# Recorded set-up, source exponentials spread by broadcast transfers, node tiles by halves and re-weighted stream keys, in a scheduled graph-attention kernel

## Chip, cores, metric

One core of one Trainium2 chip. The metric is device time of one launch in microseconds (us), the median of several runs; less is better. "Period" below is the time between the same point of two following batches in a trace (the first transpose of the last layer's attention input; batches 1 to 15).

## The reference

Sixteen independent batches of 1024 nodes with 256 channels and one adjacency matrix shared by all. Three graph-attention (GAT) layers (4, 1 and 1 heads), then 8-head attention with a feed-forward part, each on a normalised input with a residual.

```python
def gat(h, adj, W, a, alpha):                 # one head
    q = h @ W
    e = (q @ a_src)[:, None] + (q @ a_dst)[None, :]
    e = where(e >= 0, e, alpha * e)           # leaky
    return elu(softmax(where(adj > 0, e, -inf)) @ q)

for l in range(3):                            # H = 4, 1, 1
    x = x + gat_l(relu(layernorm(x)), adj)
x = x + block(relu(layernorm(x)))             # 8-head masked attention, norm, two products, norm
```

The kernel writes exp(leaky(s + d)) as a product of exponentials, so that one VectorE instruction makes a tile of weights: max(row, column) times mask. `row` holds the source exponentials of 512 nodes, the same in all 128 partitions. How `row` gets there is what the change is about.

## The kernel before

All work is recorded first, item by item, with an engine, a booked duration and the buffers read and written. A list scheduler then plays the program in its own clock, decides the order on every engine, and emits one in-order program per engine. All DMA transfers are issued by one queue (SyncE), in that order.

```python
PASS = {"pe": 0.22, "act": 0.18, "dve": 0.15, "pool": 0.13, "dma": 2.0}   # booked hand-over

def add(self, engine, us, emit, w=(), r=(), modes=("full", "full")):
    x = Work(engine, us, frozen(emit), self.base + self.pos / self.per, modes)   # key
    if engine == "pe":
        self.pos += us
    ...
def choose(e):             # lowest key among what is ready at free[e]; an item that opens
    ...                    # a ring buffer counts as ready only when a buffer is free
free[e] = at + us          # the engine's clock moves by the booked time alone
```

The rows, by four transposes on TensorE and a copy on ScalarE, for each of 12 rows of a batch:

```python
def spread(hf, h):
    g, row = r_bank.new(), r_row.new()
    pe(0.109 * TH, lambda: transposes(
            lambda k: g.t[:, k * P : (k + 1) * P],
            lambda k: e3[:, hf * TH + k, H + h : H + h + 1].to_broadcast([P, P]), TH), ...)
    act(act_us(HALF), lambda: nc.scalar.copy(row.t, g.t), [row], [g])
    return row
...
for h in range(0, H, 2):                       # layer 0: pairs of heads
    row = [spread(hf, h + u) for u in range(2)]   # the ring of rows has two buffers
```

In the same stretch of a batch the queries and keys of the attention are split into a high and a low part and stacked by small transfers, 128 of 64 KB per batch:

```python
act(act_us(HALF), lambda: nc.scalar.copy(hi.t.bitcast(F32R), sc.t), [hi], [sc])
dve(tt_us(HALF), lambda: nc.vector.tensor_sub(lo.t, sc.t, hi.t), [lo], [sc, hi])
for a in range(4):
    part = ((hi, hi, lo, lo), (hi, lo, hi, lo))[keys][a]
    for r in range(HG):
        dma(0.4, lambda: nc.sync.dma_start(              # <- booked at 0.4 us
                stack.t[a * D3 : (a + 1) * D3, r, at : at + HALF],
                part.t[r * D3 : (r + 1) * D3, :]), ...)
```

Streams set the order of preference: an item's key is its batch's number plus the TensorE time booked so far in its stream, divided by the stream's constant (`GATS, ATTENTION, FEED, AHEAD = 148.0, 110.0, 300.0, 1.0`), and the lowest key is preferred. The set-up (weights, mask) is emitted ahead of the schedule. (Cuts are marked by "..."; comments behind # are mine.)

## Time and profile before

| | before |
|---|---|
| time, median of 3 | 4728.55 us (4726.73 to 4729.57) |
| TensorE busy | 4574.2 of 4728.9 us |
| period of a batch | 286.7 us |
| start of the first attention weights | 63.1 us |

The prediction shows the lines that carry the bound. A line of this view has: line of the kernel, engine, operation, output<-inputs, shapes, count | busy us, mean ns | idle time of that engine just before them and what ended it.

```profile
L606 DVE SCALAR_TENSOR_TENSOR pt<-row,e,mask 128x512 f32<-128x512 f32 x1536 | 1071.5, 746 | 70.9 <-ACT e L540 41.7 <-ACT row L598 20.0 <-PE bank L712 5.9
...
L1024 PE MATMUL sc<-qs,ks 128*128 128x512 f32 x2048 | 822.7, 474 | 52.6 <-ACT pa L1037 20.1 <-DMA qs<-lo 16.8 <-issue 10.3
...
L702 PE MATMUL bank<-pt,qb 128*64 128x512 f32 x2048 | 529.3, 616 | 10.4 <-DVE pt L606 10.3
```

L1024 is the attention score. L606 makes the weight tiles: VectorE idled 71 us ahead of them, 20 of that for rows.

### The profile page before, as it was taken

The numbers are of one execution on the slowest core, as the hardware profiler recorded it, in microseconds if no ns is written. First come the engines' busy times: TensorE is split into PE (matmuls) and PEld (weight loads), VectorE is DVE, ScalarE is ACT, GpSimd is POOL, SyncE is SP. The second block draws the span as 40 slices with busy tenths as digits, with TensorE's granted clock in tenths as the row PEclk, the third lists the DMA queues.
The fourth block names the chain that finished last, engine by engine and source line by source line (L and its number), as shares of the span: only waits on it lengthen the run. The fifth ranks groups of instructions, "written<-read, shape, count | busy, mean of one in ns | idle before, by whom it ended". The sixth has DMA issues, their size and how long they took to land.

```text
span 4728.9 us, 67592 instructions
## 1 busy us (share of the span) xinstructions
PE 4574.2 (97%) x24898; PEld 2458.2 (52%) x24898; DVE 3400.3 (72%) x6403; ACT 2441.3 (52%) x5065; POOL 288.5 (6%) x455
## 2 busy tenths in 40 slices
PE   6899999999999999999999999999999999999997
PEld 2646456364554646546364563645546465463643
DVE  6476776867677776776777768676777767768756
ACT  2445546454554645546455464545546455464554
POOL 0000001000000000001000000000000000000000
PEclk9999999999999999999999999999999999999998
DMA  2011211102121121211212111021211212101121
GB/s 79 18 49 31 67 37 45 46 23 68 36 61 30 36 57 33 71 32 33 55 32 67 37 46 45 23 68 36 63 29 35 59 32 72 33 26 50 32 70 41
DMA packets 151234, 213.02 MB, mean 45 GB/s; under 512 B 37232, under 2 KB 71536, under 8 KB 150896
## 3 DMA queue, kind: packets, MB, share of 16 engines
q1 hardware_dynamic: 150896, 208.62, 16.2%
q8 instruction: 199, 3.26, 0.3%
q14 instruction: 139, 1.14, 0.1%
HBM read 40.70 MB, written 33.55 MB: 16 GB/s over the span
## 4 chain that ended last, share of the span: by engine, by line
PE 84%; DVE 5%; DMA 4%; SPq 4%; ACT 2%; issue 1%; POOL 0%; DVEq 0%; ACTq 0%
PE bank L632 19%; PE bank L936 19%; PE sc L1024 12%; PE bank L702 9%; PE bank L529 6%; PE bank L480 6%; PE bank L712 5%; SPq L871 3%; PE sc L850 3%; PE bank L1107 3%; DMA out_dram<-xr 2%; DVE pt L606 1%; DVE stf L423 1%; PE sc L480 1%; ACT pa L1037 1%
## 5 line engine op out<-in xcount | busy, mean ns | idle before, releaser
L1037 ACT ACTIVATE pa<-sc 128x512 f32<-128x512 f32 x2048 | 1120.4, 604 | 1018.7 <-PE sc L1024 864.4
L1045 DVE TENSOR_TENSOR pa<-pa,mask 128x1024 f32<-128x1024 f32 x1024 | 1233.4, 1221 | 446.2 <-ACT pa L1037 441.6
L606 DVE SCALAR_TENSOR_TENSOR pt<-row,e,mask 128x512 f32<-128x512 f32 x1536 | 1071.5, 746 | 70.9 <-ACT e L540 41.7
L632 PE MATMUL bank<-qb,pt 128*128 128x257 f32 x4096 | 967.2, 384 | 5.8 <-DVE pt L606 2.7
L632 PEld LDWEIGHTS bank<-qb,pt 128*128 128x128 f32 x4096 | 767.7, 190 | 234.1 <-issue 116.7
L1024 PE MATMUL sc<-qs,ks 128*128 128x512 f32 x2048 | 822.7, 474 | 52.6 <-ACT pa L1037 20.1
L1024 PEld LDWEIGHTS sc<-qs,ks 128*128 128x128 f32 x2048 | 364.3, 188 | 470.4 <-issue 165.1
L936 PE MATMUL bank<-pa,va 128*32 128x512 f32 x4096 | 546.4, 605 | 0.0
L702 PE MATMUL bank<-pt,qb 128*64 128x512 f32 x2048 | 529.3, 616 | 10.4 <-DVE pt L606 10.3
L936 PE MATMUL bank<-pa,ones 128*32 128x512 f32 x4096 | 534.1, 592 | 0.0
L529 PE MATMUL bank<-w_aug,hT 128*128 128x259 f32 (+1 forms) x1536 | 382.4, 392 | 3.7 <-ACT qb L547 2.3
L529 PEld LDWEIGHTS bank<-w_aug,hT 128*128 128x128 f32 x1536 | 284.4, 191 | 119.0 <-issue 43.5
L432 POOL TENSOR_TENSOR rstd<-rstd,neg_half 128x4 f32<-128x4 f32 x160 | 174.8, 1099 | 2389.2 <-DVE rstd L429 2275.2
L660 ACT ACTIVATE ex<-bank,rec 128x256 f32<-128x256 f32 x256 | 121.0, 472 | 342.5 <-DVE rec L652 340.0
L936 PEld LDWEIGHTS bank<-pa,ones 128*32 128x32 f32 x4096 | 133.4, 110 | 307.1 <-issue 298.5
L702 PEld LDWEIGHTS bank<-pt,qb 128*64 128x64 f32 x2048 | 132.3, 137 | 288.4 <-issue 202.9
L712 PE MATMUL bank<-pt,e 128*32 128x512 f32 x2048 | 276.8, 613 | 0.0
L850 PE MATMUL sc<-hTa,wqkv_sb 128*128 128x512 f32 x512 | 241.3, 594 | 1.5 <-ACT hTa L835 1.5
L423 DVE BATCH_NORM_STATS2 stg<-xt 128x6 f32<-128x256 f32 x512 | 212.6, 422 | 16.0 <-DMA xt<-in_x_dram 5.3
L451 ACT ACTIVATE hn<-xt,mv,rstd 128x256 f32<-128x256 f32 x384 | 205.7, 607 | 30.2 <-DVE mv L441 30.2
L936 PEld LDWEIGHTS bank<-pa,va 128*32 128x32 f32 x4096 | 83.9, 108 | 177.8 <-issue 108.5
L598 ACT COPY row<-bank 128x512 f32<-128x512 f32 x192 | 113.8, 595 | 118.0 <-PE bank L480 98.2
(105 smaller groups left out, 3876.7 us busy)
## 6 DMA issues: line engine op xcount, KB each, us to landing
ks<-hi SPq DMA_DIRECT2D x512, 64.0 KB, 2.0
ks<-lo SPq DMA_DIRECT2D x512, 64.0 KB, 2.0
qs<-hi SPq DMA_DIRECT2D x512, 64.0 KB, 2.0
qs<-lo SPq DMA_DIRECT2D x512, 64.0 KB, 2.0
xt<-in_x_dram SPq DMA_DIRECT2D x16, 1024.0 KB, 5.2
x<-xt SPq DMA_DIRECT2D x32, 512.0 KB, 2.6
xr<-x SPq DMA_DIRECT2D x64, 256.0 KB, 3.2
out_dram<-xr SPq DMA_DIRECT2D x64, 256.0 KB, 2.3
```

What stands on the lines that cost most here:

```text
L423: dve(0.342, lambda: nc.vector.bn_stats(st.t, src), [st], [src_ref])
L480: nc.tensor.transpose(dst(k), src(k), ident[:shape, :shape])
L529: nc.tensor.matmul(g.t[:, : C + 3 * H], hT.t[:, ct, k * P : (k + 1) * P], w_aug[l][:, ct, :], start=ct == 0, stop=ct == CT - 1,)
L606: lambda: nc.vector.scalar_tensor_tensor(pt.t, row.t, e3[:, jt, 2 * H + h : 2 * H + h + 1], mask[:, jt, hf * HALF : (hf + 1) * HALF], op0= ...
L632: nc.tensor.matmul(g.t[:, : D + 1], pts[jt].t[:, k * P : (k + 1) * P], qb[:, jt, 0, :], start=jt == 0, stop=jt == NT - 1,)
L702: nc.tensor.matmul(g.t[u * D : (u + 1) * D, :], qb[:, j, h + u, :], pts[u][j - jt].t, start=j == 0, stop=j == NT - 1,)
L712: nc.tensor.matmul(gd.t[c : c + D3, :], e3[:, jt + k, h + u : h + u + 1].to_broadcast([P, D3]), pts[u][k].t, start=jt == 0, stop=jt == NT - 2,
L850: nc.tensor.matmul(sc.t, wqkv_sb[:, ct, c0 : c0 + P], hT.t[:, ct, hf * HALF : (hf + 1) * HALF], start=ct == 0, stop=ct == CT - 1,)
L936: nc.tensor.matmul(accs[g, hf][den].t[r * D3 : (r + 1) * D3, :], ones if den else va.t[:, jt, f0 : f0 + D3], pas[n][r // 2].t[:, r % 2, :] ...
L1024: lambda: nc.tensor.matmul(sc.t, ks.t[:, r, jt * P : (jt + 1) * P].bitcast(F32R), q.t[:, r, :].bitcast(F32R), start=True, stop=True,),
L1037: lambda: nc.scalar.activation(pt.t[:, v, :], sc.t, AF.Exp, scale=1.0 / math.sqrt(D3)),
L1045: lambda: nc.vector.tensor_mul(pt.t, pt.t, mask[:, jt : jt + 1, i0 : i0 + HALF].to_broadcast([P, 2, HALF]),),
```

## The change

Intent: take the 768 transposes and 192 copies of the rows off TensorE and ScalarE. One transpose turns the exponentials of a half, the result is stored to DRAM, and each row is read back by a broadcast load. Also: set-up goes into the schedule, node tiles are held by halves, and the stream keys are re-weighted (VectorE work counts 0.3, each stream gets a fixed span).

```diff
+WEIGHT = {"pe": 1.0, "dve": 0.3}
...
-        x = Work(engine, us, frozen(emit), self.base + self.pos / self.per, modes)
+        stream[2] += us * WEIGHT.get(engine, 0.0)
...
+                x.key = base + span * x.pos / max(total, 1e-9)
...
-    GATS, ATTENTION, FEED, AHEAD = 148.0, 110.0, 300.0, 1.0
+    GATS, ATTENTION, FEED = (0.0, 0.965), (1.17, 0.869), (2.265, 0.313)
...  (set-up code moved into recorded items; emitted through the scheduler)
-        def spread(hf, h):
-            g, row = r_bank.new(), r_row.new()
-            pe(0.109 * TH, lambda: transposes(... e3 ... .to_broadcast([P, P]), TH), ...)
-            act(act_us(HALF), lambda: nc.scalar.copy(row.t, g.t), [row], [g])
+        def turn_rows(hf):
+            g, rt, rd = r_bank.new(), r_rt.new(), r_rd.new()
+            n = TH * H
+            pe(0.109, lambda: nc.tensor.transpose(g.t[:n, :P], e3[...], ident), ...)
+            act(0.17, lambda: nc.scalar.copy(rt.t[:n, :], g.t[:n, :P]), [rt], [g])
+            dma(0.06, lambda: nc.sync.dma_start(rd.t[:n, :], rt.t[:n, :]), [rd], [rt])
+            return rd
+        def spread(hf, h, rd):
+            row = r_row.new()
+            dma(0.8, lambda: nc.sync.dma_start(
+                    row.t.rearrange("p (t n) -> p t n", t=TH),
+                    rd.t[: TH * H, :].rearrange("(t h) n -> h t n", h=H)[h : h + 1, :, :]
+                    .partition_broadcast(P)), [row], [rd])
+            return row
...
-        b_xt = r_xt.new()           # one load of a whole batch, booked 6.0
+        xt = Halves(r_xt)           # two loads of half a batch, booked 1.6 each
```

## The prediction

> **What bounds the kernel now.** I read the page first: busy shares, then the chain that ended last.
>
> ```profile
> PE 4574.2 (97%) x24898; PEld 2458.2 (52%) x24898; DVE 3400.3 (72%) x6403; ACT 2441.3 (52%) x5065; POOL 288.5 (6%) x455
> ...
> PE 84%; DVE 5%; DMA 4%; SPq 4%; ACT 2%; issue 1%; POOL 0%; DVEq 0%; ACTq 0%
> ```
>
> TensorE is busy 97% of the span and 84% of the chain; VectorE is next at 72%. So only TensorE's own work, and what makes TensorE wait, counts. The table of windows splits the span.
>
> ```profile
> 0.00:60.00 60.00, 14.57 (x85) 10.57 (x86) 28.83 (x82) 14.84 (x21) 2.83 (x9) 1.00 0.47 155
> ...
> 640.00:926.00 286.00, 281.49 (x1539) 152.29 (x1535) 210.27 (x396) 150.76 (x314) 17.84 (x28) 0.99 0.17 45
> 926.00:1212.00 286.00, 282.29 (x1557) 152.66 (x1553) 210.88 (x397) 151.94 (x316) 17.83 (x28) 1.00 0.17 45
> ...
> 4600.00:4729.00 129.00, 102.89 (x537) 38.75 (x537) 77.06 (x125) 60.27 (x114) 5.59 (x7) 0.90 0.18 47
> ```
>
> The first busy column is TensorE. One of the 16 batches takes 286 us, of which TensorE is idle about 4. The head has 45 us without TensorE work in its first 60. The 155 us of idle in all (4728.9 - 4574.2) are head, about 60, sixteen batches at about 4, and the tail after 4500 us, about 35. The groups of instructions show what the change touches:
>
> ```profile
> L480 PE MATMUL bank<-ident,e 128*128 128x128 f32 x768 | 117.9, 277 | 0.9 <-ACT qb L547 0.8 <-ACT e L540 0.2
> ...
> L598 ACT COPY row<-bank 128x512 f32<-128x512 f32 x192 | 113.8, 595 | 118.0 <-PE bank L480 98.2 <-ACT ot L733 12.5 <-DVE pt L606 7.1
> ```
>
> 768 transposes spread the source exponentials, four for each of 192 rows, and ScalarE copies each row. Mean times of pipelined matmuls overlap, so their price is read as the step to the next start, in the timeline of TensorE:
>
> ```profile
> 2542.37 0.60 PE L480 MATMUL bank<-ident,e 128*128 128x128 f32 x4
> 2542.80 3.62 PE L885 MATMUL sc<-wqkv_sb,hTa 128*128 128x256 f32 x16
> 2548.87 0.47 PE L1024 MATMUL sc<-qs,ks 128*128 128x512 f32 x1 [2.45 <-DMA qs<-lo]
> ```
>
> Four transposes cost 0.43 us of TensorE; that is also the median over the 185 groups of four. The third line is the largest steady wait of a batch: the first score waits for the query stack, which 32 small transfers bring. Their price is in the timeline of the transfer queue:
>
> ```profile
> 2522.22 4.96 SPq L871 DMA_DIRECT2D ks<-hi  x8
> ...
> 2544.11 4.97 SPq L871 DMA_DIRECT2D qs<-lo  x8
> ```
>
> Eight take 4.96 us to issue, 0.62 us each, while the kernel's own scheduler books 0.4. Set-up, in the timeline of all engines:
>
> ```profile
> 42.82 1.00 SPq L1235 DMA_DIRECT2D xt<-in_x_dram  x2
> ...
> 53.67 2.80 PE L480 MATMUL bank<-ident,hn 128*128 128x128 f32 x8 [10.88 <-ACT hn L451]
> ...
> 63.07 1.42 DVE L606 SCALAR_TENSOR_TENSOR pt<-row,e,mask 128x512 f32<-128x512 f32 x2 [1.40 <-ACT row L598]
> ```
>
> The input is asked for only after set-up, at 42.8 us, and the first attention weights come at 63.1.
>
> **What the Trainium skill says.** "DMA: Bandwidth & Descriptors", section "Anatomy of one DMA": a transfer has a fixed part of about 2 us, mostly the receipt of the last write. The trace agrees: the 64 KB stack transfers land a median 2.0 us after issue. The same page, "Two DMAs through the same engine are not ordered": a transfer that reads what another wrote must be issued after the first one's semaphore. So the new path, store to DRAM and then broadcast load, pays two landings in series; in the trace 256 KB read back from DRAM (the residual) land in 3.2 us and 512 KB of adjacency in 3.2, so I take 2 us for the store and 2.5 to 3 for a row. "TensorE: Matmul & The Clock Gate", Part 1: after an idle window of about 3.4 us the array runs at half clock for about as long. The trace agrees: after the 10.88 us of idle above, eight transposes took 2.80 us, against 1.04 in steady state.
>
> **The change part by part.**
> Rows. Out go 192 groups of four: 192 x 0.43 = 82.6 us of TensorE. In come 96 single transposes (16 batches x 3 layers x 2 halves), at about 0.15 with their change of stream: 14.4. Net -68 us, all on the bounding engine. ScalarE loses 113.8 us and gains 96 x about 0.18 = 17; it isn't the bound. The queue gains 96 stores and 192 loads.
> Order. The streams are re-weighted. In the built program TensorE changes from one kind of matmul to another 3432 times instead of 3330. One score between two blocks of eight value matmuls costs 0.42 + 1.55 - 1.645 (half a run of 16) = 0.33 us, three cost 0.88 + 1.55 - 1.645 = 0.79: 0.23 each and 0.1 per interruption, so the extra changes cost about 5 us. TensorE's work: -63 us.
> Set-up. In the built order the input loads are the third and fourth transfers, before the adjacency, so normalisation and projections run beneath the mask work. What still gates the first attention weights are eight adjacency loads (29 us from 10.95 us on before; now from about 3), 0.77 MB of weights between them, some 7 us of small parameter loads ahead of the first row store, a store (2) and a row (3): about 44 us instead of 63, -19. But in the head nothing else fills TensorE: three changes of head pair in layer 0 and two changes of layer now each show about 2 to 4 us of row latency where a transpose and a copy took 1.4, and I give back 7. Head: -12.
> Tail. The last batch's first-half feed-forward (two blocks, 3.60 and 3.70 us) moves from amid attention to behind it, where 6.3 us of TensorE lie idle waiting for the second half's normalisation. -8.
> Halves. Node tiles of half size, three instead of two full ones twice: the next load waits for a store of the same half, 2.6 us, ahead of need; nothing on the path.
> Waits of a batch. The first score now stands after six instead of one product of layer 0, so the 2.45 us go. New waits, walked by hand through the built order from the end T of the first key projection, with 0.62 us per stack transfer: key stack from T+0.7; row store at T+6.8 once its transpose is copied; first two rows issued at T+10.3, landed at T+13.5; layer 0's first product is due at T+15.3, so it hardly waits. VectorE then makes eight weight tiles before the query remainder, which holds the second value projection about 1.5 us. The rows of the second head pair stand behind 16 query and 12 key transfers and are issued at T+32, landed at T+35 to 36; their first product is due at T+33.6 and starts at T+37: 3.3 us. In layer 1 the row store stands behind 16 query transfers: about 2 us. Together 5 to 7 us against about 4 before, so +1 to +3 a batch; I take +2 over 15 batches: +30.
> Sum: -63 - 12 - 8 + 30 = -53, so 4728.5 - 53 = 4675 us.
>
> **Rivals.**
> First: row latency fully hidden. For it: VectorE has 28% idle, weight tiles are eight deep, attention work of the batch before can fill, and VectorE's waits for rows were only 20 us. Then only 2.45 us a batch vanish (-39): -63 - 39 - 20 = -122, about 4607. Against it: layer 0's products stand in exactly the stretch where no scores are available yet.
> Second: the in-order transfer queue becomes the bound of that stretch. 128 stack transfers a batch already hold it 79 us of 286, bunched, and 18 new ones stand among them, each able to hold what is behind while it waits for a store or for VectorE. If stalls reach 9 us a batch, over 3.4 us at a time, the cold clock adds some 2 more: +7 x 15 = 105, giving about 4750.
> Third: only set-up matters, if transposes had filled slots that would otherwise idle. Against it: 97% busy and 0.9 us of idle in front of them. About 4710.
>
> **Range and chances.** The sure part is -63, give or take 5; head and tail give or take 12; the waits run from -3 to +5 us a batch, -45 to +75, and carry the spread. Eight times in ten 4628 to 4728. Two per cent faster is below 4634, which needs the waits to vanish as in the first rival: 0.18. Over 4823 would need more than the second: 0.03. Within: 0.79.
>
> **What would show it.** Transposes of the exponentials: 96, single. First attention weights near 44 us. Between the middle batches 283 to 285 us, not 286; TensorE busy about 278 of them. No wait of the first score for the query stack; instead an idle of about 3 us before a layer-0 product, put down to VectorE, which itself waits for a row's transfer. Rows landing in 2.5 to 3.2 us. I am wrong if those waits are missing and the batch takes near 279, if rows land in over 4 us, or if the batch takes 288 or more with a lower clock in the middle.

## More of the kernel before

L702 is the value product of GAT layer 0: TensorE waited 10 us for it in the whole run.

## The result, and the profile after

| | before | after |
|---|---|---|
| time, median of the same rounds | 4727.64 us | 4743.57 us (4735.61 to 4744.98) |
| ratio | | 1.0034, interval 1.0016 to 1.0051 |
| TensorE busy, profiled run | 4574.2 us | 4512.9 us |
| TensorE not busy | 154.7 us | 230.3 us |
| period of a batch | 286.7 us | 291.0 us |
| clock granted to TensorE, share of full speed | 0.990 | 0.983 |

Ratios here and below are the mean time of one kernel's fast runs over that of the other's of the same rounds, so not quite the ratio of the medians. The change counts as "same" (within 2%), but it is slower by a third of a per cent, and above the predicted range.

The page after, its busy line and the chain that ended last:

```profile
PE 4512.9 (95%) x24226; PEld 2377.5 (50%) x24226; DVE 3378.6 (71%) x6402; ACT 2355.8 (50%) x4977; POOL 327.7 (7%) x455
...
PE 67%; DVE 9%; DMA 8%; SPq 8%; ACT 4%; issue 2%; POOL 1%; DVEq 0%; ACTq 0%
```

TensorE lost 672 matmuls (24898 to 24226) and 61 us of busy time, but its part of the chain fell from 84% to 67%. Transfers (DMA) and the transfer queue's program (SPq) went from 8% together to 16%: the end is now carried in part by the queue. The windows, head and two middle batches:

```profile
0.00:60.00 60.00, 37.19 (x168) 23.04 (x170) 41.90 (x103) 18.25 (x39) 3.86 (x11) 0.89 0.51 159
641.00:932.00 291.00, 279.39 (x1514) 147.80 (x1512) 209.87 (x399) 146.60 (x310) 20.62 (x28) 0.99 0.20 55
932.00:1223.00 291.00, 279.46 (x1510) 147.34 (x1509) 208.79 (x395) 146.60 (x310) 20.61 (x28) 0.98 0.20 55
```

The head now has 37 us of TensorE work in its first 60 instead of 15. In the middle a batch takes 291 us with 279.4 busy: the idle part of a batch rose from about 4 to 11.5 us. By marks in the traces: up to the last layer of batch 0 the kernel gained 32.6 us, 8.4 more by batch 1, then lost 4.29 in each of 14 periods (60.1), and gained 4.8 behind the last mark: -32.6 - 8.4 + 60.1 - 4.8 = +14.3, the difference of the two profiled spans (4743.2 - 4728.9). The groups say what TensorE waits for:

```profile
L736 DVE SCALAR_TENSOR_TENSOR pt<-row,e,mask 128x512 f32<-128x512 f32 x1536 | 1070.0, 742 | 372.1 <-DMA row<-rd 298.8 <-PE bank L843 33.0 <-PE sc L1155 26.9
...
L1155 PE MATMUL sc<-qs,ks 128*128 128x512 f32 x2048 | 827.3, 481 | 11.4 <-ACT pa L1168 6.2 <-DMA qs<-lo 2.6 <-DVE lo L993 2.4
...
L833 PE MATMUL bank<-pt,qb 128*64 128x512 f32 x2048 | 568.0, 633 | 94.8 <-DVE pt L736 94.5
...
L1238 PE MATMUL bank<-fT,w_sb 128*128 128x512 f32 x256 | 128.3, 625 | 33.9 <-DVE yT L1276 33.3 <-ACT fT L1259 0.6
```

The score (L1155) no longer waits for its query stack, as predicted. The layer-0 product (L833) waits 94.8 us instead of 10.4, for weight tiles; and VectorE, ahead of those tiles, idles 372 us instead of 71, 299 of it for the row transfer. The product's busy time rose as well, 529.3 to 568.0, with the same 2048 matmuls: its waits slow it beyond the idle that is counted. A new wait of 33 us stands in the feed-forward (L1238), again for VectorE.

One batch in the middle, first the transfer queue (start, time, line, output<-input, count):

```profile
2236.11 4.95 SPq L1002 DMA_DIRECT2D qs<-hi  x8
2241.16 5.19 SPq L1002 DMA_DIRECT2D qs<-lo  x8
2246.47 4.32 SPq L1002 DMA_DIRECT2D ks<-hi  x7
2250.88 2.43 SPq L1002 DMA_DIRECT2D ks<-lo  x4
2253.41 0.53 SPq L720 DMA_DIRECT2D row<-rd  x1
```

then VectorE and TensorE in the same stretch:

```profile
2248.02 0.69 DVE L993 TENSOR_TENSOR lo<-sc,hi 128x512 f32<-128x512 f32 x1 [5.96 <-DMA qs<-lo]
2248.63 2.73 DVE L736 SCALAR_TENSOR_TENSOR pt<-row,e,mask 128x512 f32<-128x512 f32 x4
2257.28 1.42 DVE L736 SCALAR_TENSOR_TENSOR pt<-row,e,mask 128x512 f32<-128x512 f32 x2 [5.93 <-DMA row<-rd]
```

```profile
2252.83 1.06 PE L843 MATMUL bank<-pt,e 128*32 128x512 f32 x8
2258.09 1.97 PE L833 MATMUL bank<-pt,qb 128*64 128x512 f32 x2 [4.19 <-DVE pt L736]
```

Read from the bottom: TensorE stood 4.19 us at the product of the second head pair; the tile it needs was made at 2257.28 from a row that VectorE had awaited for 5.93 us; that row was asked for at 2253.41, behind 27 stack transfers. Two things delay it. The row buffer comes free only when VectorE has made the first pair's last tiles (a run that ends at 2251.36), and VectorE stood 5.96 us before a low part whose one buffer was still being read. And the row's place in the queue is behind those 27 transfers. Which of the two counts is a question for the experiments. The gap has an after-effect. The windows ahead of it and right behind it (last columns: granted clock, DMA share, GB/s):

```profile
2250.00:2254.00 4.00, 3.90 (x21) 1.21 (x19) 1.36 (x3) 1.17 (x2) 0.00 (x0) 1.00 0.41 100
...
2258.00:2262.00 4.00, 3.60 (x6) 0.81 (x7) 3.14 (x6) 0.00 (x0) 0.00 (x0) 0.50 0.14 35
```

The clock is 1.00 ahead of the gap and 0.50 behind it, and the two matmuls at 2258.09 took 1.97 us where the two that open the first head pair (2233.95) took 1.07. This is what the Trainium skill says in "TensorE: Matmul & The Clock Gate", Part 1, section "HAM oscillation — how this bites in real kernels": gaps of over about 3.4 us bring the half clock. The trace agrees for this gap of 4.19 us, but shorter gaps brought it too (see the last section).

### The profile page after: what moved, and what is told of

The parts are those of the page before. It is cut to its first block, busy times and chain, and to the rows that moved or that the text cites. A ratio compares the mean times of both kernels' runs of the same rounds, so it can differ in the third digit from the quotient of the medians.

```text
span 4743.2 us, 66815 instructions
## 1 busy us (share of the span) xinstructions
PE 4512.9 (95%) x24226; PEld 2377.5 (50%) x24226; DVE 3378.6 (71%) x6402; ACT 2355.8 (50%) x4977; POOL 327.7 (7%) x455
## 4 chain that ended last, share of the span: by engine, by line
PE 67%; DVE 9%; DMA 8%; SPq 8%; ACT 4%; issue 2%; POOL 1%; DVEq 0%; ACTq 0%
PE bank L763 16%; PE bank L1067 15%; PE sc L1155 9%; PE bank L833 8%; SPq L1002 7%; PE bank L639 5%; DVE pt L736 4%; PE bank L436 4%; DMA row<-rd 4%; PE bank L843 4%; PE bank L1238 3%; PE sc L981 3%; DVE pa L1176 2%; ACT hn L407 1%; ACT pa L1168 1%
## 5 line engine op out<-in xcount | busy, mean ns | idle before, releaser
L1155 PE MATMUL sc<-qs,ks 128*128 128x512 f32 x2048 | 827.3, 481 | 11.4 <-ACT pa L1168 6.2
L833 PE MATMUL bank<-pt,qb 128*64 128x512 f32 x2048 | 568.0, 633 | 94.8 <-DVE pt L736 94.5
L1155 PEld LDWEIGHTS sc<-qs,ks 128*128 128x128 f32 x2048 | 356.4, 189 | 380.7 <-ACT pa L1168 134.0
L833 PEld LDWEIGHTS bank<-pt,qb 128*64 128x64 f32 x2048 | 138.3, 140 | 399.7 <-issue 197.7
L990 ACT CAST hi<-sc 128x512 fp32r<-128x512 f32 x128 | 74.6, 583 | 311.6 <-PE sc L981 144.9
L905 ACT ACTIVATE ex<-ex 128x512 f32<-128x512 f32 x64 | 40.4, 632 | 283.6 <-DVE ex L896 283.6
```

What stands on the lines that cost most here:

```text
L833: nc.tensor.matmul(g.t[u * D : (u + 1) * D, :], qb[:, j, h + u, :], pts[u][j - jt].t, start=j == 0, stop=j == NT - 1,)
L1155: lambda: nc.tensor.matmul(sc.t, ks.t[:, r, jt * P : (jt + 1) * P].bitcast(F32R), q.t[:, r, :].bitcast(F32R), start=True, stop=True,),
```

## The experiments

Fifteen kernels ran, three rounds each, all correct, on three chips. The median of the kernel before in their rounds was 4726 to 4731 us; each ratio is to the kernel before in the same rounds.

| run | edit to the changed kernel, if not said otherwise | us | ratio to before | period |
|---|---|---|---|---|
| e1_pe_rows | rows by TensorE again | 4574.09 | 0.9675 | 278.9 |
| e2_old_keys | old stream keys | 4724.06 | 0.9991 | 288.4 |
| e3_contig | a layer-0 row is one piece in DRAM | 4718.51 | 0.9968 | 289.5 |
| e4_costs | true transfer times booked | 4516.61 | 0.9547 | 275.3 |
| e10_stack_only | stack transfer booked 0.62 | 4519.55 | 0.9561 | 275.7 |
| e11_row_only | row path booked truly, stack 0.4 | 4687.80 | 0.9914 | 287.1 |
| e8_pe_rows_costs | rows by TensorE, stack 0.62 | 4565.82 | 0.9658 | 278.6 |
| e7_pe_rows_old_keys | rows by TensorE, old keys | 4736.61 | 1.0024 | 289.1 |
| e12_before_stack | kernel before, stack 0.62 | 4713.83 | 0.9960 | 285.7 |
| e6_ring4 | four row buffers | 4593.20 | 0.9709 | 280.9 |
| e14_stack_085 | stack 0.85 | 4544.63 | 0.9602 | 276.5 |
| e15_stack_050 | stack 0.5 | 4597.27 | 0.9716 | 281.1 |
| e16_old_keys_stack | old keys, stack 0.62 | 4700.97 | 0.9938 | 286.7 |
| e17_lo2 | two low-part buffers | 4737.52 | 1.0009 | 290.9 |
| e13_contig_stack | one-piece rows, stack 0.62 | 4511.02 | 0.9532 | 275.4 |

Idle sums of TensorE told below are added up from its timeline between 350 and about 4320 us (4380 in the changed kernel, where they are 157 us).

### Which part of the change costs: e1_pe_rows and e2_old_keys

Theory: the row path's waits eat its gain. Rival: something else in the change costs.

```diff
-            dma(0.8, lambda: nc.sync.dma_start(row.t ..., rd.t ... .partition_broadcast(P)), [row], [rd])
+            pe(0.109 * TH, lambda: transposes(... e3[:, 1, hf * TH + k, h : h + 1].to_broadcast([P, P]), TH), [g, row], ...)
+            act(act_us(HALF), lambda: nc.scalar.copy(row.t, g.t), [row], [g])
```

> The changed kernel with the rows spread as before (four transposes and a copy on ScalarE); set-up, halves and streams stay changed. Theory Q (the rows' transfers are late: behind the stack transfers in the queue, and slow to land): the waits for rows go, TensorE's work grows by about 4 us a batch, the distance of two batches falls from 291.0 to 286 to 288 us, and the total is 4680 to 4710 us, because the gain of the head (about 40 us) stays. Rival S (the re-weighted streams make the waits): the waits stay beside 4 us more work, 292 us or more a batch, total above 4745.

Measured: 4574.09 us (4570.21 to 4580.37), far below what either theory gave. Idle of TensorE in the middle: 5.4 us. Its page:

```profile
PE 4495.9 (98%) x24898; PEld 2436.3 (53%) x24898; DVE 3387.4 (74%) x6402; ACT 2434.9 (53%) x5073; POOL 361.6 (8%) x455
```

The same 24898 matmuls as before take 78 us less of TensorE (4495.9 against 4574.2). So the rest of the change is worth about 154 us (3.25% by the ratio), and the rows by transfer, as scheduled, cost some 170 on top (1.0034 - 0.9675 = 3.6%). The waits in the feed-forward went with them, so they follow from the rows and need no cause of their own; how they follow, I did not trace.

```diff
-WEIGHT = {"pe": 1.0, "dve": 0.3}
+WEIGHT = {"pe": 1.0}
-    GATS, ATTENTION, FEED = (0.0, 0.965), (1.17, 0.869), (2.265, 0.313)
+    GATS, ATTENTION, FEED = (0.0, 148.0), (1.0, 110.0), (1.9, 300.0)     # and the old key formula
```

> The changed kernel with the old keys of the streams (148, 110, 300, TensorE's time alone), rows by transfers as changed. Theory Q: the waits for rows stay, as they come from the queue, 288 us or more a batch; only the waits in feed-forward (2.2 and 1.5 us a batch) may go. Rival S: idle of TensorE falls to the 4 us of before and a batch takes 283 to 284 us, total near 4640.

Measured: 4724.06 us, 0.9991 of before. The batch takes 288.4 us, as theory Q has it, but by other waits than it named:

```profile
L1155 PE MATMUL sc<-qs,ks 128*128 128x512 f32 x2048 | 810.1, 474 | 80.3 <-DMA qs<-lo 38.4
...
L833 PE MATMUL bank<-pt,qb 128*64 128x512 f32 x2048 | 551.5, 609 | 16.4 <-DVE pt L736 15.9
```

The layer-0 product waits 16.4 us instead of 94.8, and the score waits 80.3 instead of 11.4. So the stall on rows comes of the row transfers in the order that the new keys give; with the old keys it is the scores that wait. With row transfers at the wrong booking, the new keys made things 0.4% worse, which says nothing yet of the keys by themselves.

### What in the row path costs: e3_contig, e4_costs

```diff
-    rearrange("p (a t h) -> p a t h", a=3, t=NT)             # e3, and its uses
+    rearrange("p (a f h t) -> p a f h t", a=3, f=2, h=H)     # a row's four tiles side by side
```

> The changed kernel with the exponentials stored by head, so that a layer-0 row is one piece of 2 KB in DRAM instead of four of 512 B. If the four pieces are what makes a layer-0 row land in 3.9 to 4.9 us where layers 1 and 2 take 3.1 for a single one: landing about 3.1 to 3.9, the wait at the second pair of heads falls from 4.2 to about 3 us, a batch is 1 to 2.5 us shorter, total 4710 to 4730. Rival (only the place in the queue and the two landings in series count): within 5 us of the changed kernel.

Measured: 4718.51 us, 25 less than the changed kernel (ratio 0.9968, 0.9947 to 0.9989, against 1.0034). The total lies in the range of the first theory, but the wait that it was to shorten hardly moved: the idle ahead of layer 0's products went from 88.8 to 80.2 us. From the start of its request to the first tile, the first rows took 4.9 us with four 512-byte pieces and 4.2 with one of 2 KB, the second pair's first row 3.9 and 3.8. The pieces cost a little; they are not the main cause.

```diff
-            dma(0.06, ... rd <- rt)                       # store
+            dma(0.45, ...)
-                0.8, ... row <- rd
+                0.5, ..., lag=1.8 if H > 1 else 0.8       # more time until it has landed
-                        0.4,                              # stack transfer
+                        0.62,
```

> The changed kernel, its scheduler told what the trace shows of the transfers: 0.62 us to issue a stack transfer instead of 0.4, 0.45 for a row store, 0.5 for a row and 1.8 (layer 0) or 0.8 us more to land. Theory Q with a mis-booked order: the scheduler puts other work before the products that wait, layer 0 idles under 3 us instead of 7, a batch takes 284 to 287 us, total 4650 to 4690. Rival (no other work exists in that stretch): idle stays at 9 us or more a batch, total within 20 us of the changed kernel.

Measured: 4516.61 us, far below both expectations; idle in the middle 13 us, clock 0.995. Bookings alone, in a kernel whose instructions are the same and only ordered differently, are worth 4.9% of the time before. The next runs split them.

### Which booking: e10_stack_only and e11_row_only

```diff
-                        0.4,      # stack transfer
+                        0.62,
```

> Changed kernel; the scheduler is told one true figure only, that a stack transfer holds the queue 0.62 us (it booked 0.4). Rows and stores stay as it booked them. Theory A (the scheduler's clock runs ahead of the queue because 128 transfers a batch are under-booked by 0.22 us, 28 us a batch, so it thinks rows stand ready that are still queued): most of the gain of the run with all true costs comes back, 4560 to 4620. Theory B (what matters is the landing time of rows, 3.9 to 4.9 us where 2.8 was booked): little comes back, 4700 to 4745. If both are needed: 4640 to 4690.

Measured: 4519.55 us (4517.57 to 4520.45), below even theory A's range. One constant gives the whole gain. The queue in the same stretch of a middle batch:

```profile
2134.48 4.94 SPq L1002 DMA_DIRECT2D qs<-hi  x8
2139.51 3.07 SPq L1002 DMA_DIRECT2D qs<-lo  x5
2142.69 0.53 SPq L720 DMA_DIRECT2D row<-rd  x1
...
2143.91 0.52 SPq L720 DMA_DIRECT2D row<-rd  x1
```

and TensorE at the second head pair:

```profile
2147.91 1.06 PE L843 MATMUL bank<-pt,e 128*32 128x512 f32 x8
2148.91 1.94 PE L833 MATMUL bank<-pt,qb 128*64 128x512 f32 x8
```

The second pair's rows stand behind 13 query transfers instead of 27 query and key transfers, and the product starts without a wait. The reason is in the scheduler's code: a row can be chosen only when, by the scheduler's clock, a row buffer is free; until then it issues whatever stack transfers fit. 27 of them take 10.8 us in its clock and took 17.2 on the chip (2236.11 to 2253.31). It therefore puts too many ahead of the row. This was checked: run on the host, with the calls to the chip left out, the schedulers of both kernels give exactly the order of the 2336 row, store and stack transfers that the traces show. From the first pair's first row to the second pair's first row they count 16.5 us in the changed kernel, where the chip took 25.2 (2228.21 to 2253.41), and 15.2 with the true booking, where it took 15.8 (2126.93 to 2142.69). By its own clock the scheduler even holds the changed kernel to be the shorter one, with an end at 4414 us against 4434. TensorE's busy time fell too, from 4512.9 to 4443.1 us for the same 24226 matmuls: of the 226 us between the profiled spans (4743.2 and 4517.3), 156 are idle and 70 are busy time. The granted clock, 0.983 against 0.995, would account for about 54 of the 70, an estimate (1.2% of 4513).

> Changed kernel; the scheduler is told only the true figures of the new row path (store 0.45, row 0.5 of queue, 1.8 or 0.8 us more until landing); stack transfers stay booked at 0.4. Theory A (stack transfers under-booked): 4690 to 4740. Theory B (landing time of rows): 4520 to 4600. If each gives half: about 4630.

Edit: the row lines of e4 without the stack line. Measured: 4687.80 us, just under theory A's range; 67.6 us of idle ahead of the layer-0 product remain. To book the rows truly is worth a quarter of what the stack booking is worth, and adds nothing to it that shows (4516.6 and 4519.6 are of different rounds, with overlapping intervals).

### Is it the size of the error, or a lucky order: e15_stack_050 and e14_stack_085

Any change of a booking reshuffles the whole program, so a single good value proves little.

```diff
-                        0.4,
+                        0.5,      # e15; 0.85 in e14
```

> Changed kernel with stack transfers booked at 0.5 us, half way from 0.4 to what they take. If the loss grows with the error of the booking: 4580 to 4680. If only the exact figure helps or the order is chance: near 4740, or near 4520.

> Changed kernel with stack transfers booked at 0.85 us, more than the 0.62 they take. If an honest or a pessimistic booking is what helps: within 1% of 4519. If the 0.62 was a lucky order: anything between 4560 and 4750.

Measured: 4597.27 and 4544.63 us. With the booking at 0.4, 0.5, 0.62 and 0.85 the kernel takes 4743.6, 4597.3, 4519.6 and 4544.6 us: of these four, best at what the transfers take, with a mild loss when it is too high and a steep one when it is too low. Both new values fell where the theory of the error's size had put them beforehand (4580 to 4680, and within 1% of 4519). A lucky order would hardly do that.

### The row's place, or VectorE's block: e6_ring4 and e17_lo2

```diff
-    r_row = ring("row", 2, [HALF])
+    r_row = ring("row", 4, [HALF])
```

> Changed kernel with four row buffers instead of two; the booking stays wrong at 0.4. In the trace of the changed kernel the rows of the second head pair could only be asked for when VectorE had made the last weight tile of the first pair, and by then stood behind 16 query and 11 key transfers. If that place in the queue is the cause, rows that may be asked for early are issued right after the first two, and the 6.4 us a batch in front of the layer-0 product go: 4560 to 4640. If the cause is the landing time or VectorE's blocked remainder, the wait stays: 4700 to 4745.

Measured: 4593.20 us, at the wrong booking of 0.4, in the range that the place in the queue gave. The trace has the four layer-0 rows of a half issued together, ahead of the query transfers, and the idle ahead of layer 0's products is 13 us instead of 89:

```profile
2156.46 2.21 SPq L720 DMA_DIRECT2D row<-rd  x4
```

What is left (41 us ahead of the value projection, behind VectorE's low part; 18 us ahead of a value product) is another wait; I take it for the rest of the mis-ordering, which this run doesn't show. Buffers thus buy two thirds of the gain without a true clock.

```diff
-    r_lo = ring("lo", 1, [HALF])
+    r_lo = ring("lo", 2, [HALF])
```

> Changed kernel with two buffers for the low part of a query or key tile instead of one; the booking stays wrong at 0.4. In the trace VectorE stood 6 us before such a remainder until the eight transfers that read the old one had been issued, with weight tiles of the next product behind it. If that blocked remainder is the main cause: below 4620. If the row's place in the queue behind 27 stack transfers is the main cause, only the waits of the value projection go and a part of the rest: 4660 to 4730.

Measured: 4737.52 us, no gain, less than either theory gave. Queue, VectorE and TensorE of a middle batch:

```profile
2247.37 0.53 SPq L720 DMA_DIRECT2D row<-rd  x1
```

```profile
2238.10 2.74 DVE L736 SCALAR_TENSOR_TENSOR pt<-row,e,mask 128x512 f32<-128x512 f32 x4 [0.32 <-PE bank L843]
2251.32 1.42 DVE L736 SCALAR_TENSOR_TENSOR pt<-row,e,mask 128x512 f32<-128x512 f32 x2 [10.48 <-DMA row<-rd]
```

```profile
2252.13 1.55 PE L833 MATMUL bank<-pt,qb 128*64 128x512 f32 x2 [4.47 <-DVE pt L736]
```

VectorE's block before the low part is gone; the row buffer was free at 2240.84 at the latest. But the row was still asked for at 2247.37, 6.5 us later, again behind 27 query and key transfers, VectorE waited 10.48 us for it, and TensorE's gap is as long as ever. The place in the queue is the cause; VectorE's block only hid part of it.

### What the other parts are worth: e8, e7, e12, e16

> Changed kernel with the rows spread by TensorE transposes and ScalarE copies again, and the stack transfers booked at 0.62. Tells what the row transfers are worth once the schedule knows its costs: against it stands the run with row transfers and true costs, 4516.6. If TensorE's rows cost their 83 us less 14 and nothing else differs: about 4575, the same as with the old booking (4574). If the true booking helps rows by TensorE too: 4540 to 4565. If row transfers still cost waits that eat their gain: below 4530.

Edit: e1 with the stack booking of 0.62. Measured: 4565.82 us, between two of the expectations. Against e10 of the same rounds (4519.55), row transfers are worth 46 us once the queue's times are known; TensorE's busy time differs by 56 (4499.0 and 4443.1), where I had predicted 68. For rows by TensorE the booking hardly matters (4574 and 4566).

> Changed kernel with the rows by TensorE again and with the stream keys of the kernel before, so that only the recorded set-up and the half-sized node tiles are left of the change. If the re-weighted streams carry the lower time per batch of the run with rows by TensorE (278.9 against 286.7 us): here 285 to 287 per batch, 4670 to 4700 in all, with the head some 35 us shorter. If halves or set-up carry it: 279 per batch, 4570 to 4590.

Edit: e1 and e2 together. Measured: 4736.61 us, above both ranges. Set-up and halves by themselves gain nothing in the end: the mark in batch 0 comes 31 us earlier than before (191.9 and 223.2), but the period is 289.1. By the ratios (1.0024 and 0.9675) the new keys are worth 165 us where TensorE makes the rows. In this run TensorE idles 77 us in the middle, ahead of scores and layer-0 products, and a layer-0 matmul takes about 254 ns to the next start against about 235 in e1. Why the new keys have that effect I did not separate further.

```diff
-                        0.4,      # in the kernel before
+                        0.62,
```

> The kernel before with one number changed: a stack transfer is booked at 0.62 us instead of 0.4. If the true booking helps whatever stands in the queue (its first score waits for the query stack, and its layer-0 products take 246 ns a matmul against 231 where nothing waits): 4640 to 4700. If the booking matters only once rows travel by the same queue: 4715 to 4740.

Measured: 4713.83 us, 0.4% better, which just misses both expectations (the first ended at 4700, the second began at 4715). Layer 0 runs cleaner (about 241 ns a matmul instead of about 248), but 33 us of new waits for a GpSimd copy stand in its place. So the booking alone is no general gift: it is worth 0.4% here, and 4.7% (1.0034 - 0.9561) in the changed kernel, with rows in the queue and the new keys. With rows and the old keys it is worth 0.5% (e2 and e16: 0.9991 - 0.9938).

> Changed kernel with the stream keys of the kernel before and the stack transfers booked at 0.62 us. With the new keys that booking gave 4519.6. If the true booking is enough by itself: 4510 to 4550. If the re-weighted streams are needed as well (with rows by TensorE they were worth some 160 us, 4574 against 4737): 4640 to 4700.

Edit: e2 with the stack booking of 0.62. Measured: 4700.97 us, at the edge of the second expectation (4640 to 4700), so the keys are needed too. The score's group shows the wait that is left:

```profile
L1155 PE MATMUL sc<-qs,ks 128*128 128x512 f32 x2048 | 822.2, 479 | 156.2 <-DMA qs<-lo 119.0 <-ACT pa L1168 34.9 <-DVE lo L993 1.5
```

With old keys a score is due before its query stack has landed, 119 us in all. By the ratios (0.9938 and 0.9561) the new keys are worth 178 us here; at the wrong booking they cost 20. The two depend on each other.

### The best version: e13_contig_stack

> Best-version candidate: changed kernel with the stack transfers booked at 0.62 us and the layer-0 rows stored so that a row is one 2 KB piece in DRAM. One-piece rows alone were worth 25 us where TensorE waited for them. With 0.2 us a batch left of those waits: within 10 us of 4519.6. If rows' landing still stretches the layer-0 products unseen (244 ns a matmul against 231): 4490 to 4505.

Edit: e3 and e10 together. Measured: 4511.02 us, 0.9532 of before. It and e10 ran in different rounds, and their intervals overlap (0.9516 to 0.9548 and 0.9545 to 0.9577), so the piece size adds at most a little. Idle in the middle is 14 us. This is the fastest kernel, 4.7% faster than the one before and 4.9% faster than the changed one by medians.

## Why the prediction was wrong

I put 4675 us with 4628 to 4728; measured were 4743.6. The sum was -63 of TensorE work, -12 head, -8 tail, +30 waits. In the same terms the two profiles give -61 of busy time, -23 of idle before 350 us, -1 of idle behind the middle and +99 of idle in the middle, together +14.

- **TensorE's work, -63.** Busy time fell by 61.3, but the agreement is a coincidence of two errors. Where next to nothing waits (e10, 12 us of idle in the middle) the same program is busy 131 us less than before. I missed what the new keys do to TensorE's busy time (4495.9 us in e1 against 4572.5 in e7), and had booked them as a cost of 5 us for more changes of kind; the cold clock and stalls behind the new gaps, 70 us inside the busy time, hid that from the total. A part of the missed gain is the clock: its record shows 96 us at half speed in the kernel before and 48 in e10, worth about 24 us if TensorE was busy through them, an estimate. The rest stays open.
- **Head, -12.** Too small: the mark in batch 0 came 32.6 us earlier, and 31 us earlier in e7 too, so it belongs to the recorded set-up or the halves, the parts left in e7. The first weights came at 46.5 us where I had about 44, but much more of the projections and mask work ran beneath the set-up than I credited: 37 us of TensorE work in the first 60, against 15.
- **Tail, -8.** The stretch behind the last mark became 4.8 us shorter, so this was about half right.
- **Waits of a batch, +30. This is the step that failed.** TensorE's idle in the middle rose by 99 us (156.6 against 57.5), and the half clock adds its share within busy. My walk had the right actors: the score's wait goes, the rows of the second pair stand behind 16 query and about 12 key transfers, TensorE stalls at that product. The sizes were off. Per batch, over the 13.9 batches of that stretch, layer 0's products wait 6.4 us (88.8 in all) where the walk had 3.3, since a row takes 3.9 to 4.9 us from its request to the first tile there, not 2.5 to 3, and the first pair waits as well. (I had put 2.5 to 3 below the 3.2 us that the trace before shows for another 256 KB read.) The value projection waits 0.9 where I had 1.5, and layer 1 next to nothing where I had 2. Feed-forward and a value product wait 2.4 and 1.3 us (33 and 18 in all); these vanish when TensorE makes the rows, and the walk, which ended at layer 1, could not find them. VectorE's block of 5.96 us was not in the walk either, but two low-part buffers showed that it isn't the cause.
- **The deeper miss** is that I read that the scheduler books 0.4 for transfers that take 0.62, wrote it down, and used it only to correct my walk. I took the order as given and asked what it costs, and did not ask what the scheduler's wrong clock does to the order when something urgent goes through that queue in the order of the new keys. That one figure is the difference between +0.3% and -4.4%.
- **Rivals.** The second, the in-order queue as the bound of that stretch with a cold clock on top, at about 4750, named the waits that came, and my chances gave it too little; its number is luck in part, as it kept the -63, and e10 shows that the queue is no bound there once the order is right. The first, all latency hidden at about 4607, comes near to e10 and was too modest by 87 us. The third, that only set-up matters, fell with e7.
- **What would show it.** Two of the signs that I had named for being wrong came: rows in over 4 us, and a batch of 288 us or more with a lower clock.
- **A reading.** I put the 2.80 us of eight transposes after 10.88 us of idle down to the half clock alone. The first four start 0.49 us apart, as fast as ScalarE made their inputs; only the last four show the half clock, 0.213 us apart against 0.109 later. The clock of 1.00 in the first window is no reading either, since the clock record of that trace begins at 58.0 us. And "Anatomy of one DMA" is written for transfers issued by GpSimd; for SyncE's it is the measured 2.0 us that carries the argument.

## What to carry to other kernels

When a list scheduler decides the order on an in-order queue, measure how long each kind of item holds that queue and book that, before moving latency-critical work onto it; here 0.23 us too much cost 25 us, and 0.12 too little cost 78. When part of a change gives less than its arithmetic, try its parts alone: here a gain of 3.3% and a loss of 3.6%. A deeper ring lets an urgent transfer be issued early and makes the schedule less sensitive to a wrong clock (4593 instead of 4744 us).

## What the Trainium skill lacked or had wrong

- "DMA: Bandwidth & Descriptors", section "Issuing engines are not separate DMA queues", says that the sequencer's time to initiate a transfer is usually small beside the transfer. In this kernel it isn't: a 64 KB stack transfer holds the queue 0.62 us (eight in 4.95) and lands 2.0 us after its issue, a row of the second pair holds it 0.53, and 128 of the former take 79 us of a 291 us batch. To book 0.4 for 0.62 cost 224 us. I found no figure in microseconds that the page gives as the time for which one issue holds the queue.
- The same page, section "Specifications", gives 512 bytes as the least size for full rate. The runs don't measure a rate. From request to first use a row of four 512-byte pieces took 3.9 us and one of a single 2 KB piece 3.8, the first rows of a batch 4.9 and 4.2, and the kernel with single pieces was 25 us faster, so a piece of the least size was not quite free here.
- No page that I read says how much longer a 256 KB broadcast takes to land among other transfers of the same queue: 3.1 us for a lone row in layer 1, 3.9 to 4.9 among stack transfers in layer 0.
- "TensorE: Matmul & The Clock Gate", the section cited above, sets the limit for idle gaps at about 3.4 us. Here shorter gaps did it. Between 350 and 4320 us of the traces before and after, all 19 gaps of TensorE of 2.5 us or more, and 9 of the 18 between 2.0 and 2.5 us, are followed or overlapped by a stretch at half clock, of 3.41 or 6.83 us. Behind the 2.45 us gap that the prediction shows (2548.87), the window from 2549.8 to 2553.0 has a clock of 0.50, and the eight layer-0 products at 2549.27 took 3.26 us, where eight of them at 2268.85 took 1.94. So such a wait costs more than its length.
